# Reciprocals of softmax sums made on ScalarE in rows of the numerator tile, with new distances between the pipeline's stages

## The chip, the core and the metric

The kernel runs on one core of one Trainium2 chip. The core has five engines that work side by side, each with its own queue that is worked off in order: TensorE (PE; its weight loads are shown as PEld), VectorE (DVE), ScalarE (ACT), GpSimd (POOL) and SyncE (SP), which here does nothing but start DMAs. GpSimd starts the large DMAs. The metric is the device time of one execution in microseconds (us); lower is better.

## What is computed

A residual layer over 16 images of 256 channels, 28 x 28 pixels: a group norm, then two 3x3 convolutions that are each replaced by a soft table lookup, with batch norm, ReLU and a squeeze-and-excitation gate around them. The lookup is the work that counts, and it runs twice per image:

```python
def amm_conv3x3(x, centroids, w_sub, stride=1):
    B = x.shape[0]
    C, k, s = centroids.shape                                   # 256, 16, 9
    patches = jax.lax.conv_general_dilated_patches(x, (3, 3), (stride, stride), 'SAME')
...
    d = jnp.sum(p * p, axis=-1)[..., None] - 2.0 * jnp.einsum('bncs,cks->bnck', p, centroids) + jnp.sum(centroids * centroids, axis=-1)[None, None]
    attn = jax.nn.softmax(-d, axis=-1)
    lut = jnp.einsum('cks,cso->cko', centroids, w_sub)
    out = jnp.einsum('bnck,cko->bno', attn, lut)
    return out.transpose(0, 2, 1).reshape(B, -1, Ho, Wo)
...
out = amm_conv3x3(x, centroids1, wsub1, stride=1)
out = jax.nn.relu(bn_inference(out, bn1_gamma, bn1_beta, bn1_mean, bn1_var))
out = amm_conv3x3(out, centroids2, wsub2, stride=1)
out = bn_inference(out, bn2_gamma, bn2_beta, bn2_mean, bn2_var)
out = se_layer(out, se_w1, se_b1, se_w2, se_b2)
return jax.nn.relu(out + x)
```

For each channel and pixel a softmax over 16 centroids weighs the centroids; the weighted centroids (9 numbers) then go through `w_sub` into 256 output channels. All of it is float32.

## The kernel before

**Tiles.** Three channels share a strip of 32 partitions (27 rows of patch values, three rows 7, 15 and 23 for the maxima, row 30 of ones). Four strips make a tile of 128 partitions, and two such tiles make a group: 24 channels. 256 channels are 11 groups. The 784 pixels are done in two halves, 384 and 400 pixels wide. One group for one half is the work of one *slot*: 2 layers x 16 images x 2 halves x 11 groups = 704 slots. The 32 passes of one layer over one image are the *stages*, 22 slots each.

**The pipeline of one group.** `a_logits` (PE, L355) multiplies the patch tile `pt` with the centroids into four PSUM banks; `a_turn` (DVE, L371) transposes them out of PSUM into `z`, and `a_max` (DVE, L379) takes the maximum over 16 centroids into `mx`. Two groups make a *unit* (the eleventh stands alone), and per unit the maxima travel back into rows of the patch tile: `m_turn` (DVE, L388) transposes them to `mt`, `m_out` (SP, L397) writes them to DRAM (`dm`), `m_in` (SP, L406) reads them into rows 7, 15, 23 and 31 of every strip of `pt`. `b_logits` (PE, L355 again) then gives logits less their maximum, `b_exp` (ACT, L420) the exponentials `e`, `b_num` (PE, L429) the weighted centroids, `nm`, with the softmax sums in rows 7, 15, 23 and 31 of every strip, and `b_keep` (ACT, L442) copies both into `q` in SBUF. The sums then go through DRAM: `s_out` (SP, L447) writes the sum rows of `q` to `ds`, `s_in` (SP, L452) reads them spread over 128 partitions into `sp`, `r_make` (ACT, L457 and L458) makes reciprocals as exp(-ln), `r_out` (SP, L463) writes them to `dr`, and `r_in` (SP, L468) reads them into the sum rows of `rt`. `c_scale` spreads the reciprocals of a strip over its rows (DVE, L481, into `rb`) and multiplies `q` by them (POOL, L482). `c_look` (PE, L491) multiplies `q` with `w_sub` into one of two accumulators; after eleven groups ACT takes an accumulator out (L507, L517).

**What sets the order.** The order is written out by hand. `at(slot, half, f, ...)` puts a step into a table, and the program is recorded in the order of (slot, half); each engine's queue is that order cut down to its own steps. A group that starts in slot `s` has `b_logits` in slot `s + LB`, `b_num` in `s + LN`, `c_scale` in `s + LC - 1` and `c_look` in `s + LC`, with `LB, LN, LC = 3, 4, 9`; `e` is the last slot of a unit. Within a slot PE does a first logits of one group, a first half lookup of another, numerators, second logits, and the second half lookup. A PSUM ring of six banks (`p_ring`) serves the logits and numerators: the second logits of a slot take the banks that the transposes of the same slot have read.

**Beside it.** Per stage POOL prepares the patches of a coming stage: `gn_apply` (L251) for the norm, copies shifted by a pixel (L267, L269), DMAs of the image to DRAM (L273), and nine DMAs that lay out the patch tiles in DRAM (`to_pat`, `pat<-home`, L278). One DMA per unit (`patches`, `pt<-pat`, L342) brings a patch tile into SBUF, four slots ahead. Norm statistics (L220) and the final sums (L329, L330) are on DVE.

Of the kernel before, what the change touches and what calls it, by code (L numbers as in the profile page):

```python
# [8 lines left out]
F32 = mybir.dt.float32  # L9
AF = mybir.ActivationFunctionType  # L10
ALU = mybir.AluOpType
# [4 lines left out]
P = 128  # L16
# [26 lines left out]
def prow(j, s):  # L43
    base, step = PROW[j * 3 + s % 3]
    return base + step * (s // 3)
# [3 lines left out]
def kernel(  # L49
# [8 lines left out]
    ws2: bass.AP,  # L58
    nhalf: bass.AP,
    mones: bass.AP,  # L60
    vec: bass.AP,
    se_w1: bass.AP,
    se_b1: bass.AP,
# [11 lines left out]
    nc = tc.nc  # L75
# [4 lines left out]
    const = ctx.enter_context(tc.tile_pool(name="const", bufs=1))  # L80
    dram = ctx.enter_context(tc.tile_pool(name="dram", bufs=1, space=DRAM))
    drot = ctx.enter_context(tc.tile_pool(name="drot", bufs=3, space=DRAM))
    small = ctx.enter_context(tc.tile_pool(name="small", bufs=3))
# [10 lines left out]
    def view(t, off, dims):  # L94

        return bass.AP(t.tensor, t.offset + off, [list(d) for d in dims])
# [47 lines left out]
    def load(ap, name):  # L144
        t = const.tile(list(ap.shape), F32, name=name)
        nc.sync.dma_start(t, ap)
        return t
# [6 lines left out]
    ws = [load(ws1, "ws0")]  # L154
# [43 lines left out]
    ppool = ctx.enter_context(tc.tile_pool(name="ppool", bufs=5))  # L198
    tpool = ctx.enter_context(tc.tile_pool(name="tpool", bufs=4))
    epool = ctx.enter_context(tc.tile_pool(name="epool", bufs=6))  # L200
    npool = ctx.enter_context(tc.tile_pool(name="npool", bufs=4))
    rpool = ctx.enter_context(tc.tile_pool(name="rpool", bufs=2))
    mxs = [const.tile([P, 8, 32], F32, name=f"mx{i}") for i in range(2)]
    for t in mxs:
        nc.vector.memset(t, 0.0)
# [1 line left out]
    sides = {dx: const.tile([P, NB, HW], F32, name=f"side{dx}") for dx in (0, 2)}  # L207
    for t in sides.values():
        nc.gpsimd.memset(t, 0.0)


    gst = {}
# [222 lines left out]
        u["nm", gi] = bs  # L435

    def b_keep(u, gi):
        n, ng = u["px"][1], u["span"][1]
        if gi == 0:
            u["q"] = npool.tile([P, 4 * 400], F32, tag="q", name="q")  # L440
        for h, bk in enumerate(u.pop(("nm", gi))):
            nc.scalar.copy(u["q"][:, (2 * gi + h) * n : (2 * gi + h + 1) * n], bk[:, :n])  # L442

    def s_out(u):
        m = 2 * u["span"][1] * u["px"][1]
        u["ds"] = drot.tile([16, 1600], F32, tag="ds", name="ds")
        nc.sync.dma_start(view(u["ds"], 0, [[m, 16], [1, m]]), u["q"][7::8, :m])  # L447

    def s_in(u):
        m = 2 * u["span"][1] * u["px"][1] // 8  # L450
        u["sp"] = small.tile([P, 200], F32, name="sp")
        nc.sync.dma_start(u["sp"][:, :m], view(u["ds"], 0, [[m, P], [1, m]]))  # L452

    def r_make(u):
        m = 2 * u["span"][1] * u["px"][1] // 8
        sp = u["sp"][:, :m]
        nc.scalar.activation(sp, sp, AF.Ln)  # L457
        nc.scalar.activation(sp, sp, AF.Exp, scale=-1.0)  # L458

    def r_out(u):  # L460
        m = 2 * u["span"][1] * u["px"][1] // 8
        u["dr"] = drot.tile([16, 1600], F32, tag="dr", name="dr")
        nc.sync.dma_start(view(u["dr"], 0, [[m, P], [1, m]]), u["sp"][:, :m])  # L463

    def r_in(u):
        m = 2 * u["span"][1] * u["px"][1]
        u["rt"] = rts[u["n"] % 2]
        nc.sync.dma_start(u["rt"][7::8, :m], view(u["dr"], 0, [[m, 16], [1, m]]))  # L468

    MASK = [31] * 32  # L470
    for ni, r in enumerate(NROW):
# [3 lines left out]

    def c_scale(u, gi):
        n = u["px"][1]
        for h in range(2):
            a = (2 * gi + h) * n
            rb = rpool.tile([P, 400], F32, tag="rb", name="rb", bufs=3)  # L480
            nc.vector.stream_shuffle(rb[:, :n], u["rt"][:, a : a + n], MASK)  # L481
            nc.gpsimd.tensor_tensor(u["q"][:, a : a + n], u["q"][:, a : a + n], rb[:, :n], ALU.mult)  # L482

    def c_look(u, gi, o):
        l, g, n = u["l"], u["span"][0] + gi, u["px"][1]
        key = l, u["b"], u["pi"], o
        if g == 0:
            accs[key] = p_acc.tile([P, 512], F32, tag=f"acc{o}", name=f"acc{o}")
        for h in range(2):
            a = (2 * gi + h) * n  # L490
            nc.tensor.matmul(  # L491
                accs[key][:, :n], lhsT=ws[l][:, 2 * g + h, o * P : (o + 1) * P], rhs=u["q"][:, a : a + n],
                start=(g == 0 and h == 0), stop=(g == NG - 1 and h == 1),
            )
        if g == NG - 1:
            evacuate(u, o, accs.pop(key))

    accs = {}
# [20 lines left out]
                bias=sh[:, o : o + 1], scale=sc[:, o : o + 1], accum_out=ysum[:, o, pi : pi + 1],  # L519
            )  # L520

    rts = [const.tile([P, 1600], F32, name=f"rt{i}") for i in range(2)]
    for t in rts:
        nc.gpsimd.memset(t, 0.0)


    stages = [(0, 0)]
    for b in range(B):
# [1 line left out]
            stages.append((0, b + 1))  # L530
        stages.append((1, b))
    NS = 2 * NG
    LB, LN, LC = 3, 4, 9

    jobs = {}

    def at(slot, half, f, *a):
        jobs.setdefault((slot, half), []).append((f, a))

    n = nu = 0  # L540
    for si, (l, b) in enumerate(stages):
        for pi, px in enumerate(PXT):
            for g0, ng in UNITS:
                u = {"l": l, "b": b, "pi": pi, "px": px, "span": (g0, ng), "n": nu}
                nu += 1
                for gi in range(ng):
                    s = n + gi
                    at(s, 0, a_logits, u, gi)
                    at(s, 1, a_turn, u, gi)
                    at(s, 8, a_max, u, gi)  # L550
                    at(s + LB, 5, b_logits, u, gi)
                    at(s + LB, 6, b_exp, u, gi)
                    at(s + LN, 3, b_num, u, gi)
                    at(s + LN, 4, b_keep, u, gi)
                    at(s + LC - 1, 6, c_scale, u, gi)
                    at(s + LC, 2, c_look, u, gi, 0)
                    at(s + LC, 7, c_look, u, gi, 1)
                at(n - 4, 9, patches, u)
                e = n + ng - 1
                at(e, 9, m_turn, u)  # L560
                at(e, 9, m_out, u)
                at(e + 1, 4, m_in, u)
                at(e + LN, 7, s_out, u)
                at(e + LN + 1, 1, s_in, u)
                at(e + LN + 1, 7, r_make, u)
                at(e + LN + 1, 9, r_out, u)
                at(e + LN + 2, 4, r_in, u)
                n += ng
    NSLOT = n

# [9 lines left out]
    for si, (l, b) in enumerate(stages):  # L580
        t = si * NS
# [40 lines left out]
def _lay_out(inputs):  # L622

    import numpy as np

    f = lambda n: np.asarray(inputs[n], dtype=np.float32)
    x = f("x")
    bsz, ch = x.shape[:2]
    arrays = {"in_x": x.reshape(bsz, ch, -1)}
    for l in ("1", "2"):  # L630
        cent, wsub = f(_NAMES[0] + l), f(_NAMES[1] + l)
        wd = np.zeros((P, NT, 64), np.float32)
        cw = np.zeros((P, NG, 4, 32), np.float32)
        ws = np.zeros((P, NT, ch), np.float32)
        for c in range(ch):
            rt, j = divmod(c, NCH)
            t, i = divmod(rt, 4)
            g, h = divmod(t, 2)
            for s in range(9):
                r = NROW[9 * j + s]  # L640
                wd[32 * i + prow(j, s), t, K * j : K * j + K] = cent[c, :, s]
                cw[64 * h + K * j : 64 * h + K * j + K, g, i, r] = cent[c, :, s]
                ws[32 * i + r, t] = wsub[c, s]
        for h in range(2):
            for j in range(4):
                cw[64 * h + K * j : 64 * h + K * j + K, :, :, 8 * j + 7] = 1.0
        arrays["in_wd" + l], arrays["in_cw" + l], arrays["in_ws" + l] = wd, cw, ws
    nhalf = np.zeros((P, P), np.float32)
    mones = np.zeros((P, 64), np.float32)
    for i in range(4):  # L650
        nhalf[32 * i : 32 * i + 32, 32 * i + ONE] = -0.5
        for j in range(NCH):
            mones[32 * i + MROW[j], K * j : K * j + K] = -1.0
    arrays["in_nhalf"], arrays["in_mones"] = nhalf, mones
    names = [f"L0_conv_bn{l}_{v}" for l in "12" for v in ("gamma", "beta", "mean", "var")] + ["L0_conv_se_b2"]
    arrays["in_vec"] = np.stack([f(n).reshape(-1, P).T for n in names], axis=2)
    for n in ("se_w1", "se_b1", "se_w2"):
        arrays["in_" + n] = f("L0_conv_" + n)
    return {n: np.ascontiguousarray(a) for n, a in arrays.items()}, x.shape
# [17 lines left out]
```

## Time and profile before

| | |
|---|---|
| median of 2 runs | 5079.06 us (5073.65 to 5084.48) |
| the profiled execution | 5092.27 us |
| its span | 5090.5 us |
| PE busy | 4396.4 us (86%) |
| DVE busy | 3769.4 us (74%) |
| POOL busy | 2254.7 us (44%) |
| ACT busy | 2113.9 us (42%) |
| granted TensorE clock, mean | 0.919 |
| DMA moved | 885.87 MB, 174 GB/s on the mean |

The span runs from the first to the last instruction. Busy shares are means over all slots; an engine that is idle for want of another's result shows up as idle time before one of its instructions, with the one that ended it (`[4.52 <-DMA pt<-dm]`). PE's busy time grows when its clock is granted at less than full speed, so 86% is not all work. Rows of DMAs name the engine that issues them; "SPq" is SP's queue, where a row's start is the moment at which its own wait was over.

### The profile page before, as it was taken

How to read it: one execution, taken by the hardware profiler on the slowest of the kernel's cores; microseconds unless marked ns; L12 is line 12 of the kernel's file. 1: busy time of each engine (PE TensorE's matmuls, PEld its weight loads, DVE VectorE, ACT ScalarE, POOL GpSimd, SP SyncE). 2: the span in 40 equal slices, each digit the busy share in tenths (PEclk: the TensorE clock that was granted, in tenths of full speed). 3: DMA queues.
4: the chain of work that ended last, by engine and by line, in shares of the span. 5: the costliest groups of instructions: out<-in, count | busy, mean ns of one | idle time of the engine just before them, and what ended most of it. 6: DMA issues, size and time to landing. Idle time of an engine off the chain costs nothing. (4 is left out here: it accounts for less than half of the span.)

```text
span 5090.5 us, 107493 instructions
## 1 busy us (share of the span) xinstructions
PE 4396.4 (86%) x39696; PEld 1579.5 (31%) x39696; DVE 3769.4 (74%) x9144; ACT 2113.9 (42%) x5265; POOL 2254.7 (44%) x2438
## 2 busy tenths in 40 slices
PE   1788898888988889898898988889888898888988
PEld 0233333333333333233333333333233333333333
DVE  1777787677877778777787876778777787777876
ACT  0344444344444444443444443444443444434444
POOL 2444445354443545434444353544444444344433
PEclk8899999899999999998899998999989999999999
DMA  6555656556465565655556565564655656565543
GB/s 227 164 174 165 193 151 194 170 175 193 143 201 166 184 191 161 189 155 180 187 159 189 156 188 181 173 194 146 199 164 174 203 149 189 166 182 184 175 136 92
DMA packets 698762, 885.87 MB, mean 174 GB/s; under 512 B 460306, under 2 KB 565922, under 8 KB 697980
## 3 DMA queue, kind: packets, MB, share of 16 engines
q0 software_dynamic: 149248, 642.59, 38.1%
q1 hardware_dynamic: 544352, 231.75, 18.2%
q8 instruction: 313, 5.13, 0.4%
q10 hardware_dynamic: 4636, 4.66, 0.4%
q14 instruction: 213, 1.74, 0.1%
HBM read 671.90 MB, written 449.80 MB: 220 GB/s over the span
## 5 line engine op out<-in xcount | busy, mean ns | idle before, releaser
L482 POOL TENSOR_TENSOR q<-q,rb 128x384 f32<-128x384 f32 (+1 forms) x1408 | 1400.7, 1012 | 2683.7 <-DVE rb L481 1091.3
L491 PE MATMUL acc<-q,ws 128*128 128x384 f32 (+1 forms) x5632 | 2408.2, 552 | 132.6 <-POOL q L482 130.9
L371 DVE STREAM_TRANSPOSE z<-lg 128x416 f32<-128x416 f32 (+1 forms) x2816 | 1435.6, 567 | 760.8 <-PE lg L355 759.0
L355 PE MATMUL lg<-pt,wd 31*64 31x384 f32 (+2 forms) x22528 | 1536.6, 553 | 462.8 <-DMA pt<-dm 296.4
L491 PEld LDWEIGHTS acc<-q,ws 128*128 128x128 f32 x5632 | 1015.2, 201 | 1533.7 <-issue 856.3
L420 ACT ACTIVATE e<-lg 128x400 f32<-128x400 f32 (+1 forms) x2816 | 1185.8, 515 | 556.5 <-PE lg L355 555.0
L379 DVE TENSOR_REDUCE mx<-z 128x26 f32<-128x416 f32 (+1 forms) x2816 | 1396.0, 560 | 0.0
L442 ACT COPY q<-nm 128x384 f32<-128x384 f32 (+1 forms) x1408 | 613.8, 488 | 1649.6 <-issue 860.6
L355 PEld LDWEIGHTS lg<-pt,wd 31*64 31x64 f32 x22528 | 400.8, 137 | 1419.1 <-DVE z L371 424.1
L481 DVE STREAM_SHUFFLE rb<-rt 128x384 f32<-128x384 f32 (+1 forms) x1408 | 772.3, 596 | 0.9
L429 PE MATMUL nm<-e,cw 64*32 64x384 f32 (+1 forms) x11264 | 652.0, 516 | 13.1 <-ACT se_hid L299 13.1
L457 ACT ACTIVATE sp<-sp 128x192 f32<-128x192 f32 (+3 forms) x384 | 141.4, 368 | 553.4 <-DMA sp<-ds 552.0
L342 POOL DMA_DIRECT2D pt<-pat x384 | 301.0, 784 | 36.3 <-DMA pat<-home 32.6
L481 DVE LOAD_MASK_SELECT rb<-rt x1408 | 19.4, 14 | 351.2 <-DMA rt<-dr 349.7
L429 PEld LDWEIGHTS nm<-e,cw 64*32 64x32 f32 x11264 | 130.4, 106 | 434.2 <-issue 371.5
L278 POOL DMA_DIRECT2D pat<-home x288 | 244.7, 850 | 38.5 <-DMA pat<-zero 29.9
L388 DVE STREAM_TRANSPOSE mt<-mx 128x256 f32<-128x256 f32 (+1 forms) x384 | 162.4, 423 | 13.2
L458 ACT ACTIVATE sp<-sp 128x192 f32<-128x192 f32 (+3 forms) x384 | 135.4, 353 | 12.2
L251 POOL TENSOR_SCALAR xt<-xt,gn_gm,gn_rstd 128x784 f32<-128x784 f32 x32 | 96.5, 3019 | 0.1
L517 ACT ACTIVATE y<-acc,bnsh,bnsc 128x384 f32<-128x384 f32 (+1 forms) x64 | 44.2, 690 | 103.7 <-PE acc L491 103.7
L507 ACT ACTIVATE h<-acc,bnsh,bnsc 128x384 f32<-128x384 f32 (+1 forms) x64 | 44.1, 690 | 71.1 <-PE acc L491 71.1
L193 PE MATMUL sqp<-sq,nhalf_sb 128*128 128x416 f32 (+1 forms) x16 | 9.2, 743 | 62.8 <-POOL sq L191 62.8
(60 smaller groups left out, 496.8 us busy)
## 6 DMA issues: line engine op xcount, KB each, us to landing
pat<-home POOLq DMA_DIRECT2D x288, 808.5 KB, 6.4
pt<-pat POOLq DMA_DIRECT2D x160, 832.0 KB, 7.9
pt<-pat POOLq DMA_DIRECT2D x160, 768.0 KB, 5.3
home<-side POOLq DMA_DIRECT2D x64, 784.0 KB, 4.4
dm<-mt SPq DMA_DIRECT2D x640, 64.0 KB, 3.7
xt<-in_x POOLq DMA_DIRECT2D x32, 784.0 KB, 7.2
pt<-dm SPq DMA_DIRECT2D x320, 50.0 KB, 2.2
ds<-q SPq DMA_DIRECT2D x160, 100.0 KB, 2.4
```

Source lines behind the costliest of these rows:

```text
L278: nc.gpsimd.dma_start(view(pat_of(l, b), base * HW, [[32 * HW, NRT], [step * HW, 3], [1, HW]]), view(d_home[l], dx * DX + j * NPAD, [[3 * ...
L342: nc.gpsimd.dma_start(pt[:, : 2 * ng, :wn], view(pat_of(u["l"], u["b"]), 2 * g0 * P * HW + wpx, [[HW, P], [P * HW, 2 * ng], [1, wn]]),)
L355: nc.tensor.matmul(bs[i][64 * h : 64 * h + 64, :n], lhsT=wd[l][32 * i : 32 * i + rows, 2 * g + h, :], rhs=u["pt"][32 * i : 32 * i + rows, ...
L371: nc.vector.transpose(z[:, :n], u["lg", gi][i][:, :n])
L379: nc.vector.tensor_reduce(u["mx"][:, 4 * gi + i].rearrange("p (c b) -> p b c", c=2)[:, : n // 32], z[:, :n].rearrange("p (b c k) -> p b c ...
L388: nc.vector.transpose(mt[:, : 4 * ng].rearrange("p a b -> p (a b)"), u["mx"][:, : 4 * ng].rearrange("p a b -> p (a b)"))
L420: nc.scalar.activation(e[:, :n], bk[:, :n], AF.Exp, scale=2.0)
L429: nc.tensor.matmul(bs[h][32 * i : 32 * i + 32, :n], lhsT=cw[l][64 * h : 64 * h + 64, g, i, :], rhs=e[64 * h : 64 * h + 64, :n], start=True ...
L442: nc.scalar.copy(u["q"][:, (2 * gi + h) * n : (2 * gi + h + 1) * n], bk[:, :n])
L481: nc.vector.stream_shuffle(rb[:, :n], u["rt"][:, a : a + n], MASK)
L482: nc.gpsimd.tensor_tensor(u["q"][:, a : a + n], u["q"][:, a : a + n], rb[:, :n], ALU.mult)
L491: nc.tensor.matmul(accs[key][:, :n], lhsT=ws[l][:, 2 * g + h, o * P : (o + 1) * P], rhs=u["q"][:, a : a + n], start=(g == 0 and h == 0), s ...
```

## The change

The DRAM trip of the sums goes. `r_make` runs per group instead of per unit: ACT takes the logarithm of the whole numerator tile `q`, 768 or 800 values on all 128 partitions, with a per-partition scale and bias, and then exp(-x). In sum rows scale and bias are 1 and 0, in all others 0 and 1, so that those give ln(1) and then 1; the table of scales comes in as one more input (`srow`). The result `r` is what the shuffles read. `q` is now a tile per group, with five buffers instead of four of double size. The distances become `LB, LN, LC = 4, 5, 7`: second logits come a slot later, numerators too, and the lookup comes two slots behind the numerators where it came five behind. `c_scale` and `m_in` each move by one place within their slot.

```diff
-    npool = ctx.enter_context(tc.tile_pool(name="npool", bufs=4))
-    rpool = ctx.enter_context(tc.tile_pool(name="rpool", bufs=2))
+    npool = ctx.enter_context(tc.tile_pool(name="npool", bufs=5))
+    rpool = ctx.enter_context(tc.tile_pool(name="rpool", bufs=3))
...
+    srow = load(sums, "srow")
...
     def b_keep(u, gi):
-        n, ng = u["px"][1], u["span"][1]
-        if gi == 0:
-            u["q"] = npool.tile([P, 4 * 400], F32, tag="q", name="q")
+        n = u["px"][1]
+        q = npool.tile([P, 800], F32, tag="q", name="q")
         for h, bk in enumerate(u.pop(("nm", gi))):
...
-    def s_out(u):
...
-    def s_in(u):
...
-    def r_make(u):
-        m = 2 * u["span"][1] * u["px"][1] // 8
-        sp = u["sp"][:, :m]
-        nc.scalar.activation(sp, sp, AF.Ln)
-        nc.scalar.activation(sp, sp, AF.Exp, scale=-1.0)
-
-    def r_out(u):
...
-    def r_in(u):
...
+    def r_make(u, gi):
+
+        n = u["px"][1]
+        r = rpool.tile([P, 800], F32, tag="r", name="r")
+        nc.scalar.activation(r[:, : 2 * n], u["q", gi][:, : 2 * n], AF.Ln, scale=srow[:, 0:1], bias=srow[:, 1:2])
+        nc.scalar.activation(r[:, : 2 * n], r[:, : 2 * n], AF.Exp, scale=-1.0)
+        u["r", gi] = r
...
     def c_scale(u, gi):
...
+            rb = tpool.tile([P, 416], F32, tag="rb", name="rb", bufs=3)
+            nc.vector.stream_shuffle(rb[:, :n], r[:, v], MASK)
+            nc.gpsimd.tensor_tensor(q[:, v], q[:, v], rb[:, :n], ALU.mult)
...
-    LB, LN, LC = 3, 4, 9
+    LB, LN, LC = 4, 5, 7
...
-                    at(s + LC - 1, 6, c_scale, u, gi)
+                    at(s + LN + 1, 0, r_make, u, gi)
+                    at(s + LC - 1, 7, c_scale, u, gi)
...
-                at(e + 1, 4, m_in, u)
-                at(e + LN, 7, s_out, u)
-                at(e + LN + 1, 1, s_in, u)
-                at(e + LN + 1, 7, r_make, u)
-                at(e + LN + 1, 9, r_out, u)
-                at(e + LN + 2, 4, r_in, u)
+                at(e + 1, 5, m_in, u)
...
+    is_sum = (np.arange(P) % 8 == 7).astype(np.float32)
+    arrays["in_sums"] = np.stack([is_sum, 1.0 - is_sum], axis=1)
```

SP's queue in the steady part of a stage, before, at the eleventh group and the first unit after it (`dm` and `pt<-dm` are the maxima's trip; `ds`, `sp`, `dr` and `rt` that of the sums):

```order
L447 DMA ds<-q 16x1600
L397 DMA dm<-mt 64x8x32 x2
L452 DMA sp<-ds 128x200
L406 DMA pt<-dm 16x2x400 x2
L463 DMA dr<-sp 128x200
L397 DMA dm<-mt 64x4x32 x2
L468 DMA rt_174<-dr 16x1600
L406 DMA pt<-dm 16x400 x2
L447 DMA ds<-q 16x1600
L452 DMA sp<-ds 128x200
L463 DMA dr<-sp 128x200
L397 DMA dm<-mt 64x8x32 x2
```

And the same place in SP's queue with the change:

```order
L399 DMA dm<-mt 64x8x32 x2
L408 DMA pt<-dm 16x2x400 x2
L399 DMA dm<-mt 64x8x32 x2
L408 DMA pt<-dm 16x2x400 x2
L399 DMA dm<-mt 64x4x32 x2
L408 DMA pt<-dm 16x400 x2
L399 DMA dm<-mt 64x8x32 x2
```

Nothing is left on SP but the two steps of the maxima, in turn; before, either of them stood behind steps of the sums' trip.

ACT's queue in the steady part, before, two slots (`sp` is the spread sums, `nm` the numerators, `e` the exponentials):

```order
L442 COPY q<-nm 128x400 x2
L420 ACTIVATE e<-lg 128x400 x4
L442 COPY q<-nm 128x400 x2
L420 ACTIVATE e<-lg 128x400 x4
L457 ACTIVATE sp<-sp 128x200
L458 ACTIVATE sp<-sp 128x200
```

And with the change, two slots:

```order
L450 ACTIVATE r<-q,srow 128x768
L451 ACTIVATE r<-r 128x768
L443 COPY q<-nm 128x384 x2
L422 ACTIVATE e<-lg 128x384 x4
L450 ACTIVATE r<-q,srow 128x768
L451 ACTIVATE r<-r 128x768
L443 COPY q<-nm 128x384 x2
L422 ACTIVATE e<-lg 128x384 x4
```

The pair of activations comes in every slot instead of every second, is four times as wide, reads what ACT itself has written in the slot before, and stands between the exponentials of one slot and the numerators' copies of the next.

More of the change, by code (lines that the diff above doesn't have):

```diff
@@ L60 @@
     mones: bass.AP,
+    sums: bass.AP,
     vec: bass.AP,
@@ L437, in b_keep @@
     def b_keep(u, gi):
-        n, ng = u["px"][1], u["span"][1]
-        if gi == 0:
-            u["q"] = npool.tile([P, 4 * 400], F32, tag="q", name="q")
+        n = u["px"][1]
+        q = npool.tile([P, 800], F32, tag="q", name="q")
         for h, bk in enumerate(u.pop(("nm", gi))):
-            nc.scalar.copy(u["q"][:, (2 * gi + h) * n : (2 * gi + h + 1) * n], bk[:, :n])
-    def s_out(u):
-        m = 2 * u["span"][1] * u["px"][1]
-        u["ds"] = drot.tile([16, 1600], F32, tag="ds", name="ds")
-        nc.sync.dma_start(view(u["ds"], 0, [[m, 16], [1, m]]), u["q"][7::8, :m])
-    def s_in(u):
-        m = 2 * u["span"][1] * u["px"][1] // 8
-        u["sp"] = small.tile([P, 200], F32, name="sp")
-        nc.sync.dma_start(u["sp"][:, :m], view(u["ds"], 0, [[m, P], [1, m]]))
-    def r_make(u):
-        m = 2 * u["span"][1] * u["px"][1] // 8
-        sp = u["sp"][:, :m]
-        nc.scalar.activation(sp, sp, AF.Ln)
-        nc.scalar.activation(sp, sp, AF.Exp, scale=-1.0)
-    def r_out(u):
-        m = 2 * u["span"][1] * u["px"][1] // 8
-        u["dr"] = drot.tile([16, 1600], F32, tag="dr", name="dr")
-        nc.sync.dma_start(view(u["dr"], 0, [[m, P], [1, m]]), u["sp"][:, :m])
-    def r_in(u):
-        m = 2 * u["span"][1] * u["px"][1]
-        u["rt"] = rts[u["n"] % 2]
-        nc.sync.dma_start(u["rt"][7::8, :m], view(u["dr"], 0, [[m, 16], [1, m]]))
+            nc.scalar.copy(q[:, h * n : (h + 1) * n], bk[:, :n])
+        u["q", gi] = q
+    def r_make(u, gi):
[4 more added lines that the diff above has]
+        u["r", gi] = r
     MASK = [31] * 32
@@ L477, in c_scale @@
         n = u["px"][1]
+        q, r = u["q", gi], u.pop(("r", gi))
         for h in range(2):
[L479 to L482, printed above, removed]
+            v = slice(h * n, (h + 1) * n)
+            rb = tpool.tile([P, 416], F32, tag="rb", name="rb", bufs=3)
+            nc.vector.stream_shuffle(rb[:, :n], r[:, v], MASK)
+            nc.gpsimd.tensor_tensor(q[:, v], q[:, v], rb[:, :n], ALU.mult)
     def c_look(u, gi, o):
@@ L489, in c_look @@
         for h in range(2):
-            a = (2 * gi + h) * n
             nc.tensor.matmul(
-                accs[key][:, :n], lhsT=ws[l][:, 2 * g + h, o * P : (o + 1) * P], rhs=u["q"][:, a : a + n],
+                accs[key][:, :n], lhsT=ws[l][:, 2 * g + h, o * P : (o + 1) * P], rhs=u["q", gi][:, h * n : (h + 1) * n],
                 start=(g == 0 and h == 0), stop=(g == NG - 1 and h == 1),
@@ L520, in evacuate @@
             )
-    rts = [const.tile([P, 1600], F32, name=f"rt{i}") for i in range(2)]
-    for t in rts:
-        nc.gpsimd.memset(t, 0.0)
     stages = [(0, 0)]
```

## The prediction

> **What bounds the kernel now.** I read the page's busy times first, then the groups of instructions with what ended the idle time before them, then stretches of the timeline.
>
> ```profile
> PE 4396.4 (86%) x39696; PEld 1579.5 (31%) x39696; DVE 3769.4 (74%) x9144; ACT 2113.9 (42%) x5265; POOL 2254.7 (44%) x2438
> L429 PE MATMUL nm<-e,cw x11264: 482/507/847, 137.2 to 5058.8; 64*32 64x384 f32 x99, 64*32 64x400 f32 x99
> L491 PE MATMUL acc<-q,ws 128*128 128x384 f32 (+1 forms) x5632 | 2408.2, 552 | 132.6 <-POOL q L482 130.9
> L355 PE MATMUL lg<-pt,wd 31*64 31x384 f32 (+2 forms) x22528 | 1536.6, 553 | 462.8 <-DMA pt<-dm 296.4 <-DVE mx L379 43.3 <-DMA pt<-pat 38.1
> ```
>
> PE is the busiest engine. 11264 numerator matmuls at 16 a slot are 704 slots; the first starts at 137.2 us and the last near 5058.5, so 703 slots take 4921 us, 7.00 each, and 169 us lie at the two ends. PE sits idle mostly for the maxima (`pt<-dm`) and for the scaled numerators (POOL `q`). What would a slot be without those waits? A quiet stretch tells (rows of PE, ACT, DVE and POOL in order of time):
>
> ```profile
> 1931.14 0.45 DVE L388 STREAM_TRANSPOSE mt<-mx 128x256 f32<-128x256 f32 x1
> 1932.00 1.31 SPq L397 DMA_DIRECT2D dm<-mt  x2
> 1933.00 0.90 PE L429 MATMUL nm<-e,cw 64*32 64x400 f32 x16
> ...
> 1934.36 1.23 SPq L406 DMA_DIRECT2D pt<-dm  x2
> ...
> 1934.81 1.71 ACT L420 ACTIVATE e<-lg 128x400 f32<-128x400 f32 x4
> ...
> 1936.18 0.95 PE L355 MATMUL lg<-pt,wd 31*64 31x416 f32 x16
> ...
> 1937.14 2.11 DVE L371 STREAM_TRANSPOSE z<-lg 128x416 f32<-128x416 f32 x4 [0.49 <-PE lg L355]
> ...
> 1938.55 0.90 PE L429 MATMUL nm<-e,cw 64*32 64x400 f32 x16
> 1939.18 0.01 DVE L481 LOAD_MASK_SELECT rb<-rt  x1
> 1939.18 0.58 DVE L481 STREAM_SHUFFLE rb<-rt 128x384 f32<-128x384 f32 x1
> ...
> 1939.38 0.93 PE L355 MATMUL lg<-pt,wd 31*64 31x400 f32 x16
> 1939.55 0.89 ACT L442 COPY q<-nm 128x400 f32<-128x400 f32 x2 [2.37 <-PE nm L429]
> ...
> 1940.16 2.04 DVE L379 TENSOR_REDUCE mx<-z 128x26 f32<-128x416 f32 x4
> ...
> 1944.10 0.90 PE L429 MATMUL nm<-e,cw 64*32 64x400 f32 x16
> 1860.00:1890.00 30.00, 25.71 (x218) 9.15 (x218) 17.21 (x44) 13.20 (x35) 10.47 (x12) 0.89 0.68 213
> 1915.00:1940.00 25.00, 25.00 (x257) 8.90 (x256) 23.95 (x59) 12.30 (x32) 10.04 (x12) 1.00 0.55 162
> ```
>
> Numerators start at 1933.00, 1938.55 and 1944.10: a slot is 5.55 us. The last two rows are windows (busy time of PE, PEld, DVE, ACT, POOL, then granted clock, DMA share, GB/s): in the quiet one PE is busy 25.00 of 25 us at clock 1.00 and DVE 23.95, in the other PE waits and its clock is 0.89. So the floor is 703 x 5.55 = 3902 us, and 4921 - 3902 = 1019 us of the span is waits and a slowed clock. DVE, at 23.95 of 25, is close behind PE: 96% of a quiet slot.
>
> How a wait comes about, in a loaded stretch:
>
> ```profile
> 1859.29 0.45 DVE L388 STREAM_TRANSPOSE mt<-mx 128x256 f32<-128x256 f32 x1
> 1860.92 0.36 ACT L457 ACTIVATE sp<-sp 128x192 f32<-128x192 f32 x1 [7.15 <-DMA sp<-ds]
> 1861.29 1.67 PE L355 MATMUL lg<-pt,wd 31*64 31x384 f32 x16 [4.52 <-DMA pt<-dm]
> 1861.70 0.33 SPq L463 DMA_DIRECT2D dr<-sp  x1
> 1868.07 0.50 SPq L468 DMA_DIRECT2D rt<-dr  x1
> 1868.62 0.58 SPq L447 DMA_DIRECT2D ds<-q  x1
> 1869.25 1.33 SPq L397 DMA_DIRECT2D dm<-mt  x2
> SPq L468 <- DMA dr<-sp: 861.6, 291, 8.0
> SPq L463 <- ACT sp L458: 796.6, 305, 7.6
> SPq L452 <- DMA ds<-q: 716.2, 268, 7.0
> L481 DVE LOAD_MASK_SELECT rb<-rt x1408 | 19.4, 14 | 351.2 <-DMA rt<-dr 349.7
> ```
>
> The maxima are turned at 1859.74, but their write is issued only at 1869.25: SP's queue stood in `r_in` until `dr` had landed, then did `s_out`. 9.5 us are lost there, and over the run SP stands 862 + 797 + 716 us in steps of the sums' trip. That trip stalls ACT as well (552.0 us in all behind `sp<-ds`, row below), and DVE's shuffles 349.7 us, with `a_max` and `m_turn` queued behind them. So three DRAM trips feed one wait.
>
> **The change part by part.**
>
> *Four SP transfers a unit and their waits go.* SP keeps two steps, and 349.7 us of DVE stalls and 552.0 of ACT stalls lose their cause. These are no terms of the sum by themselves: they count through PE's waits.
>
> *ACT gets wide activations.* The rows nearest in kind:
>
> ```profile
> L457 ACT ACTIVATE sp<-sp 128x192 f32<-128x192 f32 (+3 forms) x384 | 141.4, 368 | 553.4 <-DMA sp<-ds 552.0
> L458 ACT ACTIVATE sp<-sp 128x192 f32<-128x192 f32 (+3 forms) x384 | 135.4, 353 | 12.2
> L328 ACT ACTIVATE y<-y,se_nb,se_gt 128x784 f32<-128x784 f32 x32 | 32.8, 1028 | 0.8 <-DVE se_nb L319 0.8
> ```
>
> L328 is 784 wide with a per-partition scale and bias, as the new Ln is: 1.03 us. The Exp has neither; bounds are L458's 0.35 (192 wide) and L328's 1.03; nearest in size is L328, and I take 0.85. A pair is 1.88 us, 704 of them 1324 us, less 277 (141.4 + 135.4): ACT rises by some 1050 to 3160 us, 4.5 of 5.55 a slot. On the path? In the quiet slot the exponentials end at 1936.52 and the next copies start at 1939.55, so ACT has 3.0 us there; the pair would end near 1938.4, and its readers, the shuffles, start at 1939.18 because DVE is in the transposes until then. Cost nothing, with 0.8 us to spare; without that cover the shuffles, and `a_max`, `m_turn` and the next slot's transposes behind them, come late, and with these the second logits, which take the transposes' banks.
>
> *Second logits a slot later.* From the end of `m_turn` at 1931.59 to its second logits at 1939.38 there are 7.8 us; a slot more makes 13.3. The trip, without SP's detours, by the landings:
>
> ```profile
> dm<-mt SPq DMA_DIRECT2D x640, 64.0 KB, 3.7
> pt<-dm SPq DMA_DIRECT2D x320, 48.0 KB, 5.1
> DMA to landing us min/median/max: 1.9/3.7/10.5
> ```
>
> The second of two issues starts 0.65 after the first, then 3.7, then 0.6 and 5.1: 10.1 us, which fits into 13.3. With the longest landing of `dm` (10.5, last row, for that tile) it is 16.9 and leaves 3.5 us of wait. Before, 296.4 us stood behind `pt<-dm` and 43.3 behind `a_max`; between 0 and 340 I take 100, since the median fits and a tail does not.
>
> *Lookup two slots behind.* `c_scale` still stands in the slot ahead of `c_look`, so POOL has what it had. The wait that stays is the norm's:
>
> ```profile
> 1995.37 5.95 POOL L251 TENSOR_SCALAR xt<-xt,gn_gm,gn_rstd 128x784 f32<-128x784 f32 x2
> ...
> 2004.31 3.02 PE L491 MATMUL acc<-q,ws 128*128 128x400 f32 x4 [2.51 <-POOL q L482]
> L329 DVE SCALAR_TENSOR_TENSOR y<-xt,gn_rstd,y 128x784 f32<-128x784 f32 x32 | 33.1, 1034 | 22.9 <-ACT y L328 21.9
> ```
>
> Sixteen times 2.51 us is 40; bounds 0 and the 131 of before. I take 65, some of it not from the norm. DVE has 4% of a slot free, 0.23 us x 703 = 163, against work outside the slots such as L329's 33.1 us; bounds 0 and 100, I take 50.
>
> *The clock.* Idle time in L355 and L491 was 463 - 38 (a wait at the start) + 133 = 558 us, the rest of the excess, 1019 - 558 = 461, is slow clock and what follows from it: 0.83 us per us waited. After the 2.51 us wait above, four lookups took 3.02 us. Remaining waits (100 + 65 + 50 = 215) are shorter; bounds 0 and 178, I take 110. The Trainium skill ("TensorE: Matmul & The Clock Gate", Part 1) has the clock drop after an idle window of about 3.4 us; here a wait of 2.51 us was already followed by lookups of nearly twice the quiet length. By the rule short waits would cost no clock and the sum would be 110 lower.
>
> *Ends.* One slot more to fill, some less to drain, against 32 us after the last numerators; between -15 and +6 I take -5. The extra load `srow` and the dropped fills are off the path (0). Buffers: `q` lives three slots and has five, patch tiles live half a unit longer with five; both hold, so 0.
>
> Sum: 3902 + 169 - 5 + 100 + 65 + 50 + 110 = 4391 us of span, against 5090.5. The profiled execution (5092.27) is 13 above the median of 5079.06, so I predict 4380.
>
> **The rivals.**
>
> *The maxima's trip stays loaded.* The large transfers (`pat<-home`, `pt<-pat`) remain, and with shorter slots the same bytes come faster: the loaded window already has the DMA engines busy 0.68 of the time, against 0.55. If landings stretch, the 340 us stay, with 115 of other waits and clock at 0.83 x 455 = 378: 4066 + 833 = 4899, less 12: 4890. Half of that growth is 4640. For it: `dm` landings up to 10.5 us. Against: 9.5 us of the loaded trip shown were SP's queue, no landing. The Trainium skill ("DMA: Bandwidth & Descriptors", "Queues, rings and completion order") speaks for this rival: a DMA's completion lands only after all earlier writes of the same DMA engine, across queues, so small transfers would still wait for the bulk ones. By that rule the time would be 4890 rather than 4380; the trace bears it out in part, since `pt<-dm` took 5.1 us there and at most 3.8 in the quiet stretch (1935.59 to 1939.38).
>
> *Slower: the new pair comes between ACT and DVE.* If Ln and Exp end after the transposes, DVE idles in every slot until `r` is there, with `a_max` and the next transposes behind. DVE works 3769.4 / 704 = 5.35 us a slot; with the whole pair exposed a slot is 5.35 + 1.88 = 7.23, 703 x 7.23 + 164 = 5247 us, 3% slower. It decides where the pair takes more than 1.88 + 0.8 = 2.7 us, or the exponentials end 0.8 later; copies of 0.69 us out of an accumulator come near, but only in two slots of eleven.
>
> *The change does nothing for PE.* If SP's stalls were only the shadow of PE's own lateness, the time is 5080 within 2%. The quiet stretch, where the same trips run without a wait, speaks against it being PE.
>
> **How the numbers follow.** About 2% is what a measurement of this kernel can tell from no change: below 4977 is faster, above 5181 slower. My forecast, 4150 (residual waits and clock of 100) to 4720 (half of the loaded rival's growth and a little more), has 0.80. Below 4150: 0.03. The loaded trip, 4720 to 4977: 0.11. No change: 0.03. Slower by the ACT pair: 0.03. So faster 0.94, same 0.03, slower 0.03, and the range is 4150 to 4720.
>
> **What would show it.** The slot between numerators should be 5.5 to 5.6 us at most places, also in loaded stretches; idle time before L355's matmuls under 200 us, mostly still `pt<-dm`; DVE's shuffles with no wait to speak of behind ACT; ACT about 3150 us busy, Ln near 1.03 and Exp near 0.85 us; granted clock over 0.96; POOL waits at the norm left. A slot of 6 us everywhere, shuffles that wait for `r`, or `pt<-dm` still above 300 us would make the prediction wrong.

## The result, and the profile after

The changed kernel took 4294.44 us (4283.44 to 4305.45, 2 runs) against 5079.06: a ratio of 0.8455, 95% interval 0.8354 to 0.8556. In four more runs, beside a kernel before of 5121.77 us, it was 4304.14 us and 0.8414 (0.8385 to 0.8443). The forecast was 4380, the range 4150 to 4720.

The page of the changed kernel: busy times, the numerators' row (its first and last start), and the groups that answer to those shown of before (same columns: busy us, mean ns | idle time before, and what ended it). The last row is of another kind, a wait: its total in us, how often, and the longest:

```profile
PE 4069.6 (95%) x39696; PEld 1481.4 (34%) x39696; DVE 3761.5 (87%) x9144; ACT 3109.7 (72%) x5905; POOL 2252.7 (52%) x2436
L431 PE MATMUL nm<-e,cw x11264: 482/507/846, 146.7 to 4280.6; 64*32 64x384 f32 x99, 64*32 64x400 f32 x99
L475 PE MATMUL acc<-q,ws 128*128 128x384 f32 (+1 forms) x5632 | 2257.8, 524 | 45.5 <-POOL q L467 44.8
L357 PE MATMUL lg<-pt,wd 31*64 31x384 f32 (+2 forms) x22528 | 1392.7, 524 | 98.9 <-DMA pt<-dm 47.3
L450 ACT ACTIVATE r<-q,srow 128x768 f32<-128x768 f32 (+1 forms) x704 | 755.9, 1074 | 0.0
L451 ACT ACTIVATE r<-r 128x768 f32<-128x768 f32 (+1 forms) x704 | 603.2, 857 | 22.4
DVE rb L466 <- ACT r L451: 17.4, 6, 3.5
```

PE is busy 95% of the span. Its busy time itself fell by 327 us with the same 39696 matmuls: the granted clock is 0.984 on the mean where it was 0.919. Idle time before the logits fell from 463 to 99 us (47 of it for the maxima; 39 more is one wait at the start, which was 38 before), before the lookups from 133 to 45. The span less its ends is 4280.3 - 146.7 = 4133.6 us, 5.88 per slot against 7.00. DVE waits for the new reciprocals 17 us in all (last row).

A slot of the second half of a stage, in order of time:

```profile
1918.08 0.90 PE L431 MATMUL nm<-e,cw 64*32 64x400 f32 x16
...
1919.90 1.71 ACT L422 ACTIVATE e<-lg 128x400 f32<-128x400 f32 x4
...
1921.45 1.09 ACT L450 ACTIVATE r<-q,srow 128x800 f32<-128x800 f32 x1
...
1922.27 2.11 DVE L373 STREAM_TRANSPOSE z<-lg 128x416 f32<-128x416 f32 x4 [0.56 <-PE lg L357]
1922.57 0.87 ACT L451 ACTIVATE r<-r 128x800 f32<-128x800 f32 x1
...
1923.73 0.90 PE L431 MATMUL nm<-e,cw 64*32 64x400 f32 x16
1924.31 0.01 DVE L466 LOAD_MASK_SELECT rb<-r  x1
...
1929.39 0.90 PE L431 MATMUL nm<-e,cw 64*32 64x400 f32 x16
```

The pair on ACT ends at 1923.44 and the shuffles start at 1924.31, when the transposes are done: 0.87 us to spare. The slot is 5.65 us. Over the whole trace (the start of every sixteenth numerator matmul, so one per slot), the median slot is 5.60 us in both kernels. What went are the long ones: 270 of the 703 slots were over 6 us before, 85 are now, and together they exceed 5.60 by 216 us where it was 1000.

### The profile page after: what moved, and what is told of

Read it like the earlier page. It is cut to its first block, busy times and chain, and to the rows that moved or that the text cites. A ratio compares the mean times of both kernels' runs of the same rounds, so it can differ in the third digit from the quotient of the medians.

```text
span 4303.8 us, 104911 instructions
## 1 busy us (share of the span) xinstructions
PE 4069.6 (95%) x39696; PEld 1481.4 (34%) x39696; DVE 3761.5 (87%) x9144; ACT 3109.7 (72%) x5905; POOL 2252.7 (52%) x2436
## 3 DMA queue, kind: packets, MB, share of 16 engines
q1 hardware_dynamic: 409328, 90.35, 10.1%
## 4 chain that ended last, share of the span: by engine, by line
PE 84%; DMA 7%; POOL 4%; DVE 3%; issue 1%; ACT 1%; SPq 0%; ACTq 0%; POOLq 0%; DVEq 0%
PE acc L475 45%; PE lg L357 27%; PE nm L431 12%; DMA dm<-mt 2%; POOL xt L253 2%; DMA pt<-dm 2%; DVE z L373 1%; DMA pat<-home 1%; DMA home<-zero 1%; POOL q L467 1%; DVE mx L381 1%; POOL side L269 1%; ACT e L422 0%; DVE rb L466 0%; DVE y L331 0%
## 5 line engine op out<-in xcount | busy, mean ns | idle before, releaser
L475 PE MATMUL acc<-q,ws 128*128 128x384 f32 (+1 forms) x5632 | 2257.8, 524 | 45.5 <-POOL q L467 44.8
L373 DVE STREAM_TRANSPOSE z<-lg 128x416 f32<-128x416 f32 (+1 forms) x2816 | 1436.8, 568 | 367.8 <-PE lg L357 361.5
L357 PE MATMUL lg<-pt,wd 31*64 31x384 f32 (+2 forms) x22528 | 1392.7, 524 | 98.9 <-DMA pt<-dm 47.3
L475 PEld LDWEIGHTS acc<-q,ws 128*128 128x128 f32 x5632 | 961.2, 190 | 1331.0 <-issue 794.2
L466 DVE STREAM_SHUFFLE rb<-r 128x384 f32<-128x384 f32 (+1 forms) x1408 | 773.5, 597 | 0.3 <-issue 0.2
L450 ACT ACTIVATE r<-q,srow 128x768 f32<-128x768 f32 (+1 forms) x704 | 755.9, 1074 | 0.0
L357 PEld LDWEIGHTS lg<-pt,wd 31*64 31x64 f32 x22528 | 362.1, 131 | 971.4 <-DVE z L373 480.2
L431 PE MATMUL nm<-e,cw 64*32 64x384 f32 (+1 forms) x11264 | 632.8, 506 | 0.0
L451 ACT ACTIVATE r<-r 128x768 f32<-128x768 f32 (+1 forms) x704 | 603.2, 857 | 22.4
L331 DVE SCALAR_TENSOR_TENSOR y<-xt,gn_rstd,y 128x784 f32<-128x784 f32 x32 | 33.2, 1036 | 39.1 <-ACT y L330 38.6
## 6 DMA issues: line engine op xcount, KB each, us to landing
pat<-home POOLq DMA_DIRECT2D x288, 808.5 KB, 6.4
```

The costliest lines, as they stand in the source:

```text
L357: nc.tensor.matmul(bs[i][64 * h : 64 * h + 64, :n], lhsT=wd[l][32 * i : 32 * i + rows, 2 * g + h, :], rhs=u["pt"][32 * i : 32 * i + rows, ...
L373: nc.vector.transpose(z[:, :n], u["lg", gi][i][:, :n])
L431: nc.tensor.matmul(bs[h][32 * i : 32 * i + 32, :n], lhsT=cw[l][64 * h : 64 * h + 64, g, i, :], rhs=e[64 * h : 64 * h + 64, :n], start=True ...
L450: nc.scalar.activation(r[:, : 2 * n], u["q", gi][:, : 2 * n], AF.Ln, scale=srow[:, 0:1], bias=srow[:, 1:2])
L451: nc.scalar.activation(r[:, : 2 * n], r[:, : 2 * n], AF.Exp, scale=-1.0)
L466: nc.vector.stream_shuffle(rb[:, :n], r[:, v], MASK)
```

## The experiments

Unless a ratio with an interval is given, a time is that of a single execution, and about 1% between two of them is noise: executions of the kernel before took 5074 to 5134 us. It took 5096 us on the chip of four of these runs (the reciprocals alone, the slot alone, the trip given time, the full extra logarithm), and medians of 5113 to 5122 on the others'.

### The two parts apart

The reciprocals without the extra slot:

```diff
-    LB, LN, LC = 4, 5, 7
+    LB, LN, LC = 3, 4, 6
```

> The change, but with the maxima's extra slot taken back: LB, LN, LC = 3, 4, 6 in place of 4, 5, 7. The sums stay on ScalarE. Theory W (the maxima's window is what counts): the window falls from 13.3 to 7.8 us, a loaded trip of about 10 us no longer fits, some 190 units wait 2.3 us and the clock adds 0.8 of that: 4600 to 5100 us, with idle time behind the maxima's DMA above 250 us. Theory S (SP's detours in the sums' trip were the whole delay of the maxima): without them the trip fits into the old window, 4300 to 4450 us.

And the extra slot in the kernel before:

```diff
-    LB, LN, LC = 3, 4, 9
+    LB, LN, LC = 4, 5, 10
```

> The kernel before, with only the distances moved by a slot: LB, LN, LC = 4, 5, 10; the sums still go through DRAM. Theory W: the waits on the maxima go, 4450 to 4700 us. Theory S: SP still stands in the sums' trip, and ACT and DVE still stall behind it, so that little is gained: 4800 to 5050 us, with DVE's wait for the reciprocals' DMA still near 350 us and ACT's for the sums' near 550.

Measured: 4702 us for the first, 5006 for the second. Of 5096, the reciprocals alone (with the new buffers and the two steps moved within their slot) take off 394 and the slot alone 90, which is not far above the noise; together they take off some 800. PE's logits in the first, the two PE groups and two waits (total, times, longest) in the second:

```profile
L357 PE MATMUL lg<-pt,wd 31*64 31x384 f32 (+2 forms) x22528 | 1466.6, 540 | 341.5 <-DMA pt<-dm 275.5 <-DMA pt<-pat 39.1 <-DVE mx L381 8.8
```

```profile
L491 PE MATMUL acc<-q,ws 128*128 128x384 f32 (+1 forms) x5632 | 2402.3, 550 | 245.4 <-POOL q L482 242.7
L355 PE MATMUL lg<-pt,wd 31*64 31x384 f32 (+2 forms) x22528 | 1520.9, 540 | 249.0 <-ACT q L442 159.6 <-DMA pt<-pat 40.5 <-DVE z L371 37.7
ACT sp L457 <- DMA sp<-ds: 949.4, 255, 14.9
DVE rb L481 <- DMA rt<-dr: 590.7, 183, 7.5
```

Without the slot the maxima's wait is 275 us, hardly less than the 296 of before, though SP no longer has any detour: the maxima's own trip, its issues and landings, overruns the old window. With the slot alone that wait is all but gone (10.9 us), and others have come in its place: ACT stands 949 us behind the spread sums (552 before), DVE 591 behind the reciprocals (350 before), and PE waits for what these two make late, 160 us for ACT's copies and 243 for POOL's products. So each part takes away one wait and the other waits then end last. The first run lies in the band of theory W, the second in that of S, though its two waits were expected to stay near 350 and 550 and grew; neither theory holds alone.

### The DRAM trip kept, but given time

The kernel before with `LB, LN, LC = 4, 5, 12`, and numerators in a tile per group to have room:

```diff
-                at(e + LN + 1, 1, s_in, u)
-                at(e + LN + 1, 7, r_make, u)
-                at(e + LN + 1, 9, r_out, u)
-                at(e + LN + 2, 4, r_in, u)
+                at(e + LN + 1, 8, s_in, u)
+                at(e + LN + 3, 0, r_make, u)
+                at(e + LN + 3, 2, r_out, u)
+                at(e + LN + 4, 5, r_in, u)
```

> The DRAM trip of the sums kept, and given time: LB, LN, LC = 4, 5, 12, with each step of the trip about a slot or more behind the step it waits for, and numerators in a tile per group (eight of them, so that the sums leave in two DMAs per unit). If only the waits in the queues of SP, ACT and DVE cost time, and neither the four transfers themselves nor anything that ScalarE's wide reciprocals do better: 4280 to 4450 us. If the transfers load the DMA engines so that the maxima's trip grows: over 4550 us, with over 150 us of idle time behind the maxima's DMA.

Measured: 4574 us, over the first band and in the second's time, but not for the second's reason. PE's logits, and the waits (the first is PE's for the maxima):

```profile
L355 PE MATMUL lg<-pt,wd 31*64 31x384 f32 (+2 forms) x22528 | 1516.0, 528 | 156.0 <-ACT q L441 83.2 <-DMA pt<-pat 39.2 <-DVE z L371 17.0
PE lg L355 <- DMA pt<-dm: 14.9, 11, 6.6
SPq L406 <- DMA dm<-mt: 814.2, 371, 9.2
ACT sp L458 <- DMA sp<-ds: 594.7, 156, 13.0
DVE rb L482 <- DMA rt<-dr: 368.7, 144, 10.6
```

Only 15 us stand behind the maxima's DMA. ACT and DVE still stall behind the trip, 595 and 369 us. Its steps share SP's queue with `m_in`, which stands 814 us until the maxima's write has landed; in the 6 us ahead of an `s_in` that ACT then waited for, SP had stood in `m_in` for 1.6 us on the mean, ahead of the other `s_in` for 0.5. So the shared queue has a part in it; that it is the whole cause is not shown, since SP stood in `s_in`'s own wait, for the landing of `ds`, longer too (1.2 against 0.7 us). Two thirds of the gain (522 of 802) came from the time given all the same.

### The trip as a ghost

What do the trip's transfers cost if no engine waits for them? To the changed kernel the four steps were added again, from rows of `r` and back into a tile that nobody reads:

```diff
+                    at(s + LN + 1, 6, s_out, u, gi)
...
+                at(e + LN + 2, 1, s_in, u)
+                at(e + LN + 2, 9, r_out, u)
+                at(e + LN + 3, 4, r_in, u)
```

> The change, with the trip through DRAM added again as a ghost: rows of r go out, come in spread, go out and come back by four steps on SP with their waits (the first in two DMAs per unit), but no engine reads what arrives. SP's detours and the transfers' load are back, the stalls of ACT and DVE behind the trip are not. If the stalls of ACT and DVE were the cost that the extra slot alone could not remove: 4290 to 4380 us, with under 100 us of idle time behind the maxima's DMA. If SP's detours and the load cost by themselves: over 4500 us, with over 150 us behind the maxima's DMA.

Measured: 4763 us, 340 us behind the maxima's DMA, so the second case. The same without the extra slot (`LB, LN, LC = 3, 4, 6`):

> The same ghost trip without the extra slot for the maxima (LB, LN, LC = 3, 4, 6); beside the run without ghost and without slot (4702 us, 275 us behind the maxima's DMA). If SP's detours are what made the maxima late in the old window: over 4950 us and over 400 us behind the maxima's DMA. If the landings alone overrun the old window: 4700 to 4800 us, and 270 to 330 us.

Measured: 4909 us, 402 us behind the maxima's DMA; in time between the two bands, nearer to the first, in the wait in the first:

```profile
PE lg L357 <- DMA pt<-dm: 402.0, 137, 10.8
```

And with the extra slot and every step reading something fixed, so that none waits for another (two of the four lines that differ):

```diff
-        nc.sync.dma_start(u["sp"][:, :m], view(u["ds"], 0, [[m, P], [1, m]]))
+        nc.sync.dma_start(u["sp"][:, :m], zeros([[0, P], [1, m]]))
...
-        nc.sync.dma_start(rts[u["n"] % 2][7::8, :m], view(u["dr"], 0, [[m, 16], [1, m]]))
+        nc.sync.dma_start(rts[u["n"] % 2][7::8, :m], zeros([[0, 16], [1, m]]))
```

> The ghost trip's transfers without its waits: the same number and sizes of DMAs at the same places of SP's queue, with the maxima's extra slot, but each reads something fixed (weights in SBUF, a row of zeros and ones in DRAM), so that no step waits for another. Beside the ghost trip with waits (4763 us, 340 us behind the maxima's DMA) and none at all (4304 us, 45 us). If the waits in SP's queue are the cost: 4300 to 4450 us and under 110 us behind the maxima's DMA. If the load on the DMA engines and SP's issuing time are: 4600 to 4800 us and over 220 us. In between, the share of each can be read off.

Measured: 4555 us, between the two bands in time, and 223 us behind the maxima's DMA. PE's logits and the largest waits on SP, first of the ghost with waits (with the slot), then of the ghost without:

```profile
L357 PE MATMUL lg<-pt,wd 31*64 31x384 f32 (+2 forms) x22528 | 1475.2, 538 | 409.8 <-DMA pt<-dm 339.5 <-DMA pt<-pat 40.4 <-DVE z L373 12.0
SPq L465 <- DMA ds<-r: 779.7, 246, 5.6
SPq L474 <- DMA dr<-sp: 538.9, 231, 7.3
ACT r L450 <- DMA ds<-r: 64.2, 26, 7.5
```

```profile
L357 PE MATMUL lg<-pt,wd 31*64 31x384 f32 (+2 forms) x22528 | 1428.9, 531 | 283.4 <-DMA pt<-dm 222.9 <-DMA pt<-pat 38.3 <-DVE z L373 10.9
SPq L408 <- DMA dm<-mt: 1027.1, 316, 10.8
```

With the slot in all four, the times are 4304 (no trip), 4555 (its transfers), 4763 (and its waits on SP), 5006 (and ACT and DVE standing behind it, the run with the slot alone). So of some 702 us between the ends, about 251 go with the transfers and SP's time to issue them, 208 with the waits in SP's queue and 243 with the stalls of ACT and DVE. These are differences of single executions (but for the first) on three chips, taken in one order of several; the ghost has one DMA more per unit and stands about a slot later than the true trip, its waits held ACT for 64 us, and the last run also lacks the wide reciprocals and has other distances. The three sizes are good to some tens of us at best.

Nor are the 251 us a fixed price of these transfers. The run with the trip given time had the same slot for the maxima and as many transfers of the same sizes, and PE waited 15 us for the maxima there, against 223 in the ghost without waits. Its steps stood at other places of SP's queue, and other waits held PE up first; which of the two makes the difference is not shown. Load and issuing time were not tried apart by a run; what the trace tells of them is in the last section.

### ACT's margin

The changed kernel with the logarithm done twice, and, in another run, with its first half done twice (the first writing is overwritten with the same values); the edit of the full one:

```diff
+        nc.scalar.activation(r[:, : 2 * n], u["q", gi][:, : 2 * n], AF.Ln, scale=srow[:, 0:1], bias=srow[:, 1:2])
         nc.scalar.activation(r[:, : 2 * n], u["q", gi][:, : 2 * n], AF.Ln, scale=srow[:, 0:1], bias=srow[:, 1:2])
```

> The change with the logarithm done twice (the second writes the same result): the pair on ACT grows from 1.93 to 3.0 us. By the margin read from the quiet slot (0.8 us between the pair's end and the shuffles) the shuffles come 0.3 us late in every slot, with the maxima and the next transposes behind them: 4450 to 4550 us, with DVE waiting for r over 100 us. If DVE and PE have slack that takes it up: 4290 to 4340 us.

> The change with half of the logarithm done twice (one extra activation 384 or 400 wide, about 0.7 us): the pair grows from 1.93 to 2.6 us, under the margin of 2.7 read from the quiet slot. If that margin holds: DVE waits for r under 60 us and the time is within 25 us of the change (4280 to 4330 us, a ratio of 0.836 to 0.847). If what counts is ACT's load as such (72% busy, then 83%): half of what the full second logarithm cost, 35 to 50 us more, and DVE's wait near 100 us.

Measured: 4384 us for the full one and 4309.3 for the half one, whose ratio to the kernel before is 0.8441 (0.8407 to 0.8475), not to be told from the change's own. DVE's wait for `r` in the one and the other:

```profile
DVE rb L467 <- ACT r L452: 213.6, 460, 4.2
```

```profile
DVE rb L467 <- ACT r L452: 58.4, 70, 3.9
```

The margin holds: 0.7 us more on ACT in every slot cost nothing that can be measured, and 1.04 us more made DVE wait 213.6 / 704 = 0.30 us a slot, the 0.3 that was read off. The time rose by only some 80 to 95 us (4384 against 4304, or 0.860 against 0.841 of the kernel before on its chip), since DVE makes part of that up before PE needs its transposes (DVE's own wait for PE's logits fell from 361.5 to 239.3 us). Both of the full run's bands were missed, from between.

### What is left

The changed kernel once more, beside three edits of it:

> The changed kernel once more, on the chip of the three runs that are compared with it: 4280 to 4320 us.

The norm's two passes on POOL in two places of a slot (`gn_apply` with `k` as an argument):

```diff
-            for k, f in enumerate((gn_stats, gn_mean, gn_var, gn_apply)):
+            for k, f in enumerate((gn_stats, gn_mean, gn_var)):
                 at(t0 + 2 + k, 9, f, b)
+            at(t0 + 5, 2, gn_apply, b, 0)
+            at(t0 + 5, 9, gn_apply, b, 1)
```

> The change, with the norm's two passes over the image (3.0 us each on POOL, in one piece before) put into two places of the slot: one ahead of the scaling, one behind. If the lookups' wait for POOL at that slot is real cost: it falls from 3.2 us to about 0.2 in 14 images, and with the clock that follows the time falls by 40 to 70 us. If another wait takes its place at once (POOL's shifts and DMAs queue behind in any case): within 15 us of the change.

Yet a slot more for the maxima:

```diff
-    ppool = ctx.enter_context(tc.tile_pool(name="ppool", bufs=5))
+    ppool = ctx.enter_context(tc.tile_pool(name="ppool", bufs=6))
...
-    LB, LN, LC = 4, 5, 7
+    LB, LN, LC = 5, 6, 8
```

> The change with yet one slot more for the maxima: LB, LN, LC = 5, 6, 8, and six patch tiles in place of five. If the waits that are left behind the maxima's DMA (47 us on the matmuls, 30 on the weight loads) are the tail of the trip's length: they go to under 10 us and the time falls by 50 to 100 us. If the slots 10 to 12 of a stage are long because DVE is late there (final sums of an image) and the maxima only leave late: the wait moves to DVE's transposes and the time stays within 20 us.

And both:

> The two edits together, the version that should be the fastest: if both causes are separate costs, 90 to 160 us less than the change (4130 to 4210 us); if they hide each other, no more than the better of the two.

| kernel | us, median of 4 | ratio to the kernel before (95%) |
|---|---|---|
| the change again | 4304.14 | 0.8414 (0.8385 to 0.8443) |
| norm in two places | 4268.77 | 0.8347 (0.8315 to 0.8378) |
| yet a slot more | 4254.89 | 0.8315 (0.8287 to 0.8344) |
| both | 4216.09 | 0.8246 (0.8222 to 0.8270) |

PE's wait that the first edit is about, and the one that the second is about:

```profile
PE acc L475 <- POOL q L467: 23.7, 15, 1.7
```

```profile
PE lg L357 <- DMA pt<-dm: 6.9, 5, 2.2
```

The wait for POOL halved, from 44.8 to 23.7 us, and did not fall to nothing; 35 us came of it, a little under what was expected. The executions of one kernel differ by up to 29 us, so these sizes are rough. The maxima's tail went from 45 to 7 us and 49 us with it, just under its band. Together they give 88 us: 35 + 49 = 84, so the causes look separate, though 88 is a little short of the 90 expected. The version with both is faster than either kernel that was compared here, by 17.5% and 2%.

## Why the prediction was right

The sum was 4391 us of span against 4303.8 measured, and most of its terms can be held against the profile.

*The floor* of 5.55 us a slot, 3902 us, was the right one to take: the rows above show 5.65 in the second half of a stage, the median over all slots is 5.60, and the excess over 3902 fell from 1019 to 232 us. The sum had 325 for it. *Waits on the maxima* were set at 100 and are 47; *waits for POOL* at 65, and are 45. For DVE and clock together 160 were set, and 232 - 92 = 140 are left for them. A granted clock of 0.984 over 4303.8 us is some 70 us lost, where 110 were set; the price of 0.83 us per us waited gives 0.83 x 92 = 76, so that price held and the waits it was put on were set too high. The other 70 stay with DVE and with slots of 5.60 and 5.65 in place of 5.55. *The ends* are 146.7 + 23.3 = 170 us where 164 were set. So the sum lay 87 us too high: 53 and 20 for the two waits and 40 for the clock, less 20 for DVE and 6 for the ends. No two large errors met by luck. Of the signs named ahead one held only in part: of the 99 us before the logits half, and not most, are the maxima's.

*The sum without a clock cost* (110 less, 4281) comes nearer as a number, but its reason does not hold here. In the trace of the changed kernel TensorE ran for 143 us at half clock. Such a stretch began during, or within 3.5 us after, 11 of 14 PE waits of 3.0 to 3.4 us, and in the kernel before with 25 of 28 waits of 2.5 to 3.0 us (waits in the first 200 us left out).

*ACT* came out as worked: 3110 us busy (3160 forecast), the logarithm 1.07 us (1.03), the exponential 0.86 (0.85). That it is hidden, and by how much, was tried with the half and the full extra logarithm, and both fit a margin of 0.8 us: 0.7 us more was hidden, 1.04 us more was not. The slower rival, the pair between ACT and DVE, needed more than that.

*The loaded rival* kept its premise and lost its conclusion. The median landing of the maxima's write did not fall (the profile gives it for 192 of the 768 writes):

```profile
DMA to landing us min/median/max: 2.2/4.2/18.0
```

It was 3.7 us before. That is what one would see by the rule of the Trainium skill named there ("DMA: Bandwidth & Descriptors", "Queues, rings and completion order"), that a small transfer's completion stands behind the bulk writes: these stayed, and the landing with them. No run here takes the bulk writes away, so the rule itself was not tried. But the longer window took the landing in, as the forecast had it, up to a tail of 47 us. One reading behind this rival was wrong: 5.1 us, set against 3.8 in the quiet stretch, is the median of the 48 KB reads over the whole run and not of a loaded stretch, and the 50 KB reads have less than half of it:

```profile
pt<-dm SPq DMA_DIRECT2D x320, 50.0 KB, 2.2
```

The trip of 10.1 us was worked out with 5.1; with 2.2 the same sum is 7.2 us.

Three things in the working were off. First, "9.5 us are lost there", in SP's queue, was given as the reason why the maxima came late. It is one of two: without any detour and with the old window they waited 275 us instead of 296, because the maxima's trip overran the window by itself. Second, the removed transfers were given no price as load; the ghost puts it, with the issuing time and at its places in the queue, near 250 us. Third, "the change does nothing for PE" and the other rivals treated the two parts as one; apart they give 394 and 90 us, and 320 of the 800 come only when both are there. None of these moved the sum, because it was built from the quiet slot and what would be left, not from the waits that go.

## What to carry to other kernels

Where a fixed order keeps one engine near full, price a change from the quiet stretch upward: the slot that the profile shows without waits, plus the waits that will remain, since the waits that go overlap and don't add up. A DRAM trip of small transfers cost in three places here: in the time to move and issue it, in its waits in the queue of the engine that issues it, and in the queues of the engines that wait for it. One slot more for the maxima alone moved the waits to the next place and gained 90 us; more distance for every step of the trip gained 522, taking the trip away 802. Work put on an engine with time to spare was free up to a margin that can be read from one slot of the timeline: the end of the new work against the moment at which its reader is ready anyway.

## What the runs showed of the hardware that was not expected

The four steps of the ghost without waits, of about 100 KB each, raised the median landing of the maxima's 64 KB writes only from 4.2 to 4.8 us (the profile gives a quarter and an eighth of them), and that of the 808.5 KB layout transfers from 6.4 to 7.5, and yet the time went from 4304 to 4555, with PE waits of up to 12.3 us behind the maxima. What grew was the time until SP got to the maxima's write. From the end of `m_turn` to the start of `m_out` nine tenths of the 384 units took at most 3.3 us in the change and 7.1 in the ghost; from there to the start of `m_in` it was 6.9 and 7.3. Where the write left more than 0.5 us late, the delays add up to 239 and 705 us. In these SP stood 160 and 326 us in `m_in` for an earlier landing, and issued the ghost's steps for 223 us, at 0.3 to 0.6 us and more for one. So much of the cost in this trace is that SP comes late to the maxima's write; how much of it slower landings cause is open, since no run took the one without the other. The rows, first of the change, then of the ghost without waits:

```profile
pat<-home POOLq DMA_DIRECT2D x288, 808.5 KB, 6.4
dm<-mt SPq DMA_DIRECT2D x640, 64.0 KB, 4.2
```

```profile
pat<-home POOLq DMA_DIRECT2D x288, 808.5 KB, 7.5
dm<-mt SPq DMA_DIRECT2D x640, 64.0 KB, 4.8
PE lg L357 <- DMA pt<-dm: 222.9, 47, 12.3
```
